# A convolution and attention kernel: the branches' sum gets its own tile, and two readers of GpSimd's results move back in the queue

## The chip, the cores and the metric

The kernel runs on one core of a Trainium2 chip. The metric is the device time of one execution in microseconds (us), the median of several. A core has five engines that matter here, each with a queue of its own that it works off in order: PE (TensorE, matrix products), DVE (VectorE), ACT (ScalarE), POOL (GpSimd) and SP (SyncE, which here only issues DMAs). An instruction whose inputs or whose buffer are not ready waits, and everything behind it on its engine waits with it.

## The reference

The input x is (8, 256, 64, 64) in f32. Two layers follow one another, each on a group-normalised x and with a residual sum. Layer 0 makes 3x3 weights for every point out of 1x1 convolutions and sums nine shifted value maps with them. Layer 1 adds two things: a 7x7 local attention, and a dynamic convolution, nine branches of two depthwise 3x3 convolutions, weighted by a softmax over the branches:

```python
wts = jnp.einsum('oc,bchw->bohw', Wfc, x).reshape(b, C, kc2, h, w)
wts = jax.nn.softmax(wts, axis=2)
...
hid = jax.nn.relu(_dwconv(xr, w1))
oc = _dwconv(hid, w2).reshape(b, kc2, C, h, w)
out_conv = jnp.sum(oc * wts.transpose(0, 2, 1, 3, 4), axis=1)
return rate1 * out_att + rate2 * out_conv
```

The nine branches of the reference are equal before they are weighted, since xr is x broadcast to nine copies. The kernel computes the depthwise result oc once for each channel. It computes eight exponentials of differences to the ninth branch's logits, with S their sum, and multiplies oc by (S + 1) / (S + 1), which in this case is 1 up to rounding. The change leaves all of this arithmetic as it is.

## The kernel before, in words

An image has eight bands of eight rows (512 points); a band has its 256 channels in two halves (ct = 0, 1) of 128 partitions. The main loop goes over the 64 bands g of all images, band by band, and over eight steps s in each band: steps 0 to 3 belong to ct = 0, steps 4 to 7 to ct = 1. A step of layer 1 treats two 8x8 tiles of queries for its half: scores (L699, on PE), masked maxima (L708, DVE), exponentials (L716, ACT), the reciprocal of their sums (L723, DVE), probabilities (L725, ACT), transposes (L731, PE, and L733, ACT), weighted values (L743, PE), and their addition to the output tile xr (L753, DVE). The scores and the weighted values of a step lie in one PSUM tile with the tag "sco", which has one buffer: the next step's scores need L753 to be done.

The same step computes two of the eight branches' logits (L821, PE) and exponentials (L826, ACT) into the two planes of an "ex" tile, tag "ex" with three buffers. POOL sums these tiles over the four steps of a half (L1017, after the second, third and fourth step). DVE works off the depthwise taps of the same half (L778, L804), eight per convolution.

At the end of a half, ACT copies the depthwise result from PSUM to a tile "oc" (L814), and dynamic_sum finishes the half: POOL adds the two planes (L832), DVE adds 1 and caps (L839), takes the reciprocal in two parts (L840, L844), POOL weighs (L849 to L851: sum by reciprocal, oc by that, added to xr), and after the second half SP stores xr.

While layer 1 works on band g, layer 0 prepares the bands g + 10 to g + 12: small_maps and value_maps (PE, and ACT in step 0 and 1), hidden maps, and tap_weights, whose nine products per band are made by DVE (L451) and summed by POOL (L461), two buffers of the tag "prod". The last product's sum is added to the band of x (L464), and "take" measures its statistics (L491, DVE, two bn_stats) and stores it as x1. The first layer's bands run out ten bands before the end.

The order of all queues is written out by hand. A step has six places. Code that stands in the step itself is issued at its place, and `after(n, f)` issues f n places later, ahead of what the step issues there, and in the order in which such calls were made:

```python
def after(n, f):
    later.append((place[0] + n, f))
```

Places are only an order in the queues; nothing waits for a place. In a band of 48 places, counted from step 0: ex tiles are added at places 14, 20 and 26 for the first half and at 38, 44 and 50 for the second (50 is place 2 of the next band). L832 stands at 26 and 50, behind the ex add there. The quotient (L839, L840) stands five places on, at 31 and 55 (step 5 and step 1, place 1 of the step: ahead of two taps and of L723), the second reciprocal (L844) at 34 and 58, the weighing at 36 and 60, the store at 66. The products 0 to 8 stand at 12, 13, 18, 24, 25, 28, 36, 37 and 42, each followed at once by POOL's add (product 0 has none). The copy of old keys (L628, POOL) stands at 14 and 38, the position sums (L616, POOL) at 32; in the bands next to an image's border these come one step earlier. The statistics of take stand seven places after product 8, at 49, which is place 1 of step 0 of the next band.

Of the kernel before, what the change touches and what calls it, by code (L numbers as in the profile page):

```python
# [10 lines left out]
F32 = mybir.dt.float32  # L11
# [7 lines left out]
P = 128  # L19
# [5 lines left out]
BAND = R * W  # L25
# [61 lines left out]
def conv_layers_kernel(ctx: ExitStack, tc: tile.TileContext, ins: dict, out: bass.AP):  # L87
    nc = tc.nc
# [93 lines left out]
    w1 = ctx.enter_context(tc.tile_pool(name="l1", bufs=2))  # L182
# [32 lines left out]
    def after(n, f):  # L215
        later.append((place[0] + n, f))
# [148 lines left out]
    def pieces(v, q):  # L365

        return v.rearrange("(g s) n -> g s n", s=SHARE)[:, :, q * PIECE : (q + 1) * PIECE]
# [61 lines left out]
    def tap_weights(b, i, u, alone, at):  # L429


        im = images[b]
        pw = ps.tile([P, TG, SR * HP], F32, tag="gen", name=f"pw_{b}_{i}_{u}", bufs=5)
        for j in range(TG):
            nc.tensor.matmul(  # L435
                pw[:, j], c2[:, TG * u + j], h2n[i % 2].rearrange("p r c -> p (r c)"), start=True, stop=True
            )

        def product(j):
            k = TG * u + j  # L440
            if alone and j == TG - 1:
                prod = w1.tile([P, NCT, RP, W], F32, tag="yp", name=f"prod_{b}_{i}_{k}", bufs=3)
                prod = prod.rearrange("p t r c -> p (t r c)")[:, : SHARE * SR * HP]
                prod = prod.rearrange("p (s n) -> p s n", s=SHARE)
            else:
                prod = w0.tile(
                    [P, SHARE, SR * HP], F32, tag="prod" if k else "sum", name=f"prod_{b}_{i}_{k}",
                    bufs=2 if k else 1,
                )
            at = k // 3 * HP + k % 3  # L450
            nc.vector.scalar_tensor_tensor(  # L451
                prod[:, :, :RUN], pw[:, j, :RUN].unsqueeze(1).to_broadcast([P, SHARE, RUN]),
                par[:, PCB2 + k : PCB2 + k + 1],
                im.x3q[i].rearrange("p s r c -> p s (r c)")[:, :, at : at + RUN], ALU.add, ALU.mult,
            )
            if k == 0:
                im.sum = prod
            elif alone and j == TG - 1:
                after(5, lambda: gather(prod))
            else:  # L460
                nc.gpsimd.tensor_add(im.sum[:, :, :RUN], im.sum[:, :, :RUN], prod[:, :, :RUN])  # L461
            if k == KK - 2 + (not alone):
                x = im.xg[i]
                nc.gpsimd.tensor_add(x, x, rows(im.sum))  # L464
                if alone:
                    after(8, combine)
                after(20 if alone else 7, take)

        def rows(v):
            return v.rearrange("p s (r c) -> p s r c", c=HP)[..., :W]  # L470

        def gather(prod):
            if u == 0:
                im.part = score_tile(f"sum_{b}_{i}").rearrange("p t (s r c) -> p t s r c", r=SR, c=W)
            for t in range(2):
                nc.tensor.matmul(
                    im.part[:, t], ident, rows(prod)[:, t * SHARE // 2 : (t + 1) * SHARE // 2],
                    start=(u == 0), stop=(u == KK // TG - 1),
                )

        def combine():
            x = im.xg[i].rearrange("p s r c -> p (s r c)")
            nc.vector.tensor_add(x, im.part.rearrange("p t s r c -> p (t s r c)"), x)

        def take():
            x = im.xg[i]
            if i == 0:
                im.st1 = stat.tile([P, 2 * NB, 6], F32, tag="st1", name=f"st1_{b}")
            for t in range(2):
                v = x[:, t * SHARE // 2 : (t + 1) * SHARE // 2].rearrange("p s r c -> p (s r c)")  # L490
                nc.vector.bn_stats(im.st1[:, 2 * i + t, :], v)  # L491
            t = im.x1[i] = dram.tile([C, BAND], F32, tag="x1", name=f"x1_{b}_{i}")
            for q in range(NQR):
                v = x[q * REL : (q + 1) * REL].rearrange("p s r c -> p s (r c)")
                nc.sync.dma_start(out=pieces(t, q), in_=v)

        for j, n in enumerate(at):
            after(n, lambda j=j: product(j))
# [186 lines left out]
    def score_tile(nm):  # L685

        return ps.tile([P, 2, 512], F32, tag="sco", name=f"sco_{nm}")
# [25 lines left out]
    def exponentials(nm, prob, nmax):  # L713
        tot = w1.tile([P, 2], F32, tag="tot", name=f"tot_{nm}", bufs=4)
        for h in range(2):
            nc.scalar.activation(  # L716
                prob[:, h, :NKEY], prob[:, h, :NKEY], AF.Exp, bias=nmax[:, h : h + 1], scale=-1.0,
                accum_out=tot[:, h : h + 1],
            )
        return tot  # L720
# [89 lines left out]

    def depthwise_end(b, i, ct, acc):

        oc = w1.tile([P, BAND], F32, tag="oc", name=f"oc_{b}_{i}_{ct}")
        nc.scalar.activation(oc, acc.rearrange("p r c -> p (r c)"), AF.Copy, scale=rate2)  # L814
        return oc

# [10 lines left out]

    def dynamic_sum(b, i, ct, ex, oc):

        tot = ex[:, 1]  # L830
        xr = images[b].xr[i]
        nc.gpsimd.tensor_add(tot, tot, ex[:, 0])  # L832
        rec = w1.tile([P, BAND], F32, tag="rec", name=f"rec_{b}_{i}_{ct}", bufs=1)
        n = BAND // 2

        def quotient():


            nc.vector.tensor_scalar(tot, tot, 1.0, 1.0e37, ALU.add, ALU.min)  # L839
            nc.vector.reciprocal(rec[:, :n], tot[:, :n])  # L840
            after(3, second)

        def second():
            nc.vector.reciprocal(rec[:, n:], tot[:, n:])  # L844
            after(2, weigh)

        def weigh():

            nc.gpsimd.tensor_mul(tot, tot, rec)  # L849
            nc.gpsimd.tensor_mul(oc, oc, tot)  # L850
            nc.gpsimd.tensor_add(xr[:, ct], xr[:, ct], oc)  # L851
            if ct == NCT - 1:
                after(6, store)

        def store():
            nc.sync.dma_start(
                out=out[b].rearrange("(t p) n -> p t n", p=P)[:, :, i * BAND : (i + 1) * BAND], in_=xr
            )

        after(5, quotient)  # L860


    def beside(g, s):
# [93 lines left out]
    with tc.manual_schedule():  # L957
# [20 lines left out]
        for g in range(-AHEAD, B * NB):  # L978
            b, i = divmod(g, NB)
            for s in range(STEPS):  # L980
                ct, m = divmod(s, NT // 2)
                mid, end = beside(g, s)
                steer(g, s)
                if g >= 0:
# [4 lines left out]
                    tot = exponentials(nm, prob, nmax)  # L989
                advance()  # L990
                if g >= 0:
                    ex, exb = w1.tile([P, 2, BAND], F32, tag="ex", name=f"ex_{nm}", bufs=3), ex if m else None
# [21 lines left out]
                if g >= 0:  # L1014
                    branch_weights(b, i, ct, m, 1, ex)
                    if exb is not None:
                        after(4, lambda ex=ex, exb=exb: nc.gpsimd.tensor_add(ex, ex, exb))  # L1017
                    if m == 1:
                        conv[1]()
                        conv = depthwise_middle(b, i, ct)  # L1020
                    if m == NT // 2 - 1:
                        oc = depthwise_end(b, i, ct, conv[1])
                        after(4, lambda a=(b, i, ct, ex, oc): dynamic_sum(*a))
# [93 lines left out]
```

## Time and profile before

The median of three runs is 4419.8 us (4418.06 to 4427.21). The profiled execution has a span of 4415.5 us at a granted TensorE clock of 0.989.

| engine | busy | share of the span |
|---|---|---|
| PE, matmuls | 4191.5 us | 95% |
| PE, weight loads | 2116.2 us | 48% |
| DVE | 3586.4 us | 81% |
| ACT | 3041.2 us | 69% |
| POOL | 3005.2 us | 68% |

The DMA engines are busy for about a third of the time, and the data comes from HBM at 82 GB/s over the span. Layer 1 begins about 300 us into the span. Between 330 and 3330 us PE is busy for about 974 of every 1000 us; from 3860 us on, where layer 0's products have run out, for 536 of 540 us, and POOL falls from 72% to 48% of the time.

| group | engine | count | mean of one |
|---|---|---|---|
| L461 product into the sum, 128x1040 | POOL | 485 | 2412 ns |
| L1017 ex tiles, 128x1024 | POOL | 384 | 2361 ns |
| L832, L849, L850, L851, 128x512 | POOL | 128 each | 1269 to 1276 ns |
| L839 sum plus one, capped, 128x512 | DVE | 128 | 1123 ns (median 423, longest 3076) |
| L840, L844 reciprocals, 128x256 | DVE | 128 each | 1753, 1746 ns |
| L491 statistics, 128x512 | DVE | 128 | 684 ns |
| L451 product, 128x1040 | DVE | 576 | 1280 ns |

How to read this: a group's mean counts only the time in which the instruction ran, not the time for which it waited. What an engine waited for stands in the list of waits and, in the timeline, in brackets behind an instruction: the idle time of the engine just before it and the instruction that ended it. Bands are nearly equal in length: 64.9 us for bands 1, 2, 4 and 5 of an image, 72.0 for band 0, 67.6 for band 3 (where the next image's weights of layer 0 are scaled), 62.9 and 63.4 for bands 6 and 7, by the starts of the first score matmuls.

### The profile page before, as it was taken

The page shows a single profiled execution, that of the slowest core. Times are in us where ns is not written, and L with a number is a line of the kernel's source. Part 1 is how long each engine was busy: PE and PEld are TensorE (multiplying, and loading weights), DVE is VectorE, ACT ScalarE, POOL GpSimd, SP SyncE. Part 2 cuts the span into 40 slices and gives each one's busy share as a digit, 9 for nine tenths or more (in the row PEclk, how much of TensorE's full clock was granted, in tenths as well). Part 3 has the DMA queues.
Part 4 walks back from the last instruction along what each step waited for, and adds up shares of the span by engine and source line. Part 5 has one row for each costly group of instructions (what it writes and reads, how often), then busy time and mean ns, then how long its engine had stood idle before and what let it go on. Part 6 is the DMA issues. An engine that isn't in the chain of part 4 may idle for free.

```text
span 4415.5 us, 72043 instructions
## 1 busy us (share of the span) xinstructions
PE 4191.5 (95%) x25004; PEld 2116.2 (48%) x25004; DVE 3586.4 (81%) x7244; ACT 3041.2 (69%) x7598; POOL 3005.2 (68%) x1778
## 2 busy tenths in 40 slices
PE   5679999999999999999999999999999999999998
PEld 2334445544454444544445444554445444454444
DVE  5658888888888888888888888888888888877777
ACT  2246777776677776777777676776777776677776
POOL 3657767677777677767777776767777777844444
PEclk9889999999999999999999999999999999999999
DMA  6662423423332332333332342342332332211100
GB/s 190 155 155 69 104 69 78 109 80 76 101 88 70 101 90 69 98 95 77 88 91 77 88 104 63 82 110 69 84 92 60 80 95 56 55 43 34 37 29 20
DMA packets 381259, 367.90 MB, mean 83 GB/s; under 512 B 55392, under 2 KB 282720, under 8 KB 380640
## 3 DMA queue, kind: packets, MB, share of 16 engines
q1 hardware_dynamic: 377568, 358.68, 31.6%
q8 instruction: 198, 3.24, 0.3%
q10 hardware_dynamic: 3328, 4.62, 0.3%
q14 instruction: 165, 1.35, 0.1%
HBM read 261.48 MB, written 101.71 MB: 82 GB/s over the span
## 4 chain that ended last, share of the span: by engine, by line
PE 60%; DVE 18%; POOL 11%; issue 4%; ACT 1%; DMA 1%; SPq 0%; POOLq 0%; DVEq 0%; ACTq 0%
PE pf L821 27%; POOL prod L461 6%; PE sco L743 5%; PE pk L653 4%; PE p L357 4%; DVE prod L451 4%; PE ptp L731 4%; PE sco L699 4%; PE pq L632 3%; POOL ex L1017 3%; DVE acc L778 3%; PE pvt L602 3%; DVE ex L839 2%; DVE acc L804 2%; PE p L325 2%
## 5 line engine op out<-in xcount | busy, mean ns | idle before, releaser
L821 PE MATMUL pf<-yp,c_wfc 128*128 128x512 f32 x4096 | 1988.2, 608 | 1.4
L461 POOL TENSOR_TENSOR prod<-prod,prod 128x1040 f32<-128x1040 f32 x485 | 1170.1, 2412 | 238.7 <-DVE prod L451 212.1
L826 ACT ACTIVATE ex<-pf 128x512 f32<-128x512 f32 x1024 | 606.7, 592 | 545.5 <-PE pf L821 309.2
L1017 POOL TENSOR_TENSOR ex<-ex,ex 128x1024 f32<-128x1024 f32 x384 | 906.7, 2361 | 75.7 <-ACT ex L826 71.0
L821 PEld LDWEIGHTS pf<-yp,c_wfc 128*128 128x128 f32 x4096 | 698.5, 190 | 534.9 <-issue 490.8
L778 DVE SCALAR_TENSOR_TENSOR acc<-yp,c_chan,acc 128x504 f32<-128x504 f32 (+3 forms) x1104 | 765.0, 693 | 55.3 <-ACT acc L769 35.0
L451 DVE SCALAR_TENSOR_TENSOR prod<-pw,c_par,x3q 128x1040 f32<-128x1040 f32 x576 | 733.8, 1280 | 71.2 <-PE pw L435 29.2
L849 POOL TENSOR_TENSOR ex<-ex,rec 128x512 f32<-128x512 f32 x128 | 163.4, 1276 | 902.7 <-DVE rec L844 845.2
L804 DVE SCALAR_TENSOR_TENSOR acc<-hid,c_chan,acc 128x504 f32<-128x504 f32 (+3 forms) x1024 | 757.8, 740 | 18.6 <-ACT acc L798 0.6
L725 ACT ACTIVATE prob<-prob,tot 128x196 f32<-128x196 f32 x1024 | 411.8, 451 | 400.6 <-DVE tot L723 400.6
L716 ACT ACTIVATE prob<-prob,nmax 128x196 f32<-128x196 f32 x1024 | 462.0, 455 | 96.8 <-DVE nmax L708 96.3
L743 PEld LDWEIGHTS sco<-pt,vt 112*64 112x64 f32 x8176 | 282.0, 137 | 368.0 <-issue 126.7
L753 DVE SCALAR_TENSOR_TENSOR xr<-sco,bv,xr 128x128 f32<-128x128 f32 x511 | 174.5, 341 | 309.2 <-PE sco L743 309.0
L708 DVE CUSTOM_DVE_ANT_0 prob<-sco,c_mask 128x196 f32<-128x196 f32 x1024 | 324.3, 354 | 77.8 <-PE sco L699 76.9
L743 PE MATMUL sco<-pt,vt 112*64 112x64 f32 x8176 | 350.9, 228 | 35.0 <-DVE nmax L708 32.7
L699 PE MATMUL sco<-kb,qb 64*64 64x196 f32 x4096 | 295.1, 357 | 51.3 <-DVE xr L753 51.0
L731 PE MATMUL ptp<-ident,prob 128*112 128x128 f32 x2044 | 332.3, 285 | 0.0
L733 ACT COPY pt<-ptp 112x512 f32<-112x512 f32 x511 | 295.6, 579 | 30.1 <-PE ptp L731 29.9
L731 PEld LDWEIGHTS ptp<-ident,prob 128*112 128x112 f32 x2044 | 206.7, 133 | 152.3 <-issue 82.8
L558 PE MATMUL pv<-yp,c_wv 128*128 128x512 f32 (+2 forms) x576 | 251.7, 562 | 0.0
L653 PE MATMUL pk<-yp,c_wk 128*128 128x512 f32 (+2 forms) x576 | 245.0, 553 | 0.0
L357 PE MATMUL p<-xc,w3s 128*128 128x512 f32 x512 | 244.9, 602 | 0.0
(134 smaller groups left out, 5527.6 us busy)
## 6 DMA issues: line engine op xcount, KB each, us to landing
x<-x3n SPq DMA_DIRECT2D x128, 264.0 KB, 2.1
x3q<-x SPq DMA_DIRECT2D x128, 264.0 KB, 6.9
xc<-in_x SPq DMA_DIRECT2D x64, 512.0 KB, 5.3
xg<-in_x SPq DMA_DIRECT2D x256, 128.0 KB, 5.1
x<-xg SPq DMA_DIRECT2D x256, 128.0 KB, 2.4
yp<-x SPq DMA_DIRECT2D x128, 256.0 KB, 3.2
xr<-x SPq DMA_DIRECT2D x64, 512.0 KB, 5.7
out_x<-xr SPq DMA_DIRECT2D x64, 512.0 KB, 3.1
```

Source lines behind the costliest of these rows:

```text
L451: nc.vector.scalar_tensor_tensor(prod[:, :, :RUN], pw[:, j, :RUN].unsqueeze(1).to_broadcast([P, SHARE, RUN]), par[:, PCB2 + k : PCB2 + k + 1],
L461: nc.gpsimd.tensor_add(im.sum[:, :, :RUN], im.sum[:, :, :RUN], prod[:, :, :RUN])
L653: nc.tensor.matmul(pk[:, :n], wk[:, kt, ct * P : (ct + 1) * P], im.yp[i][:, kt, a : a + n], start=(kt == 0), stop=(kt == NCT - 1),)
L699: nc.tensor.matmul(sco[half[t], h, :NKEY], qb[half[h], 2 * m + t].rearrange("p r c -> p (r c)"), kb[half[h], :, c0 : c0 + KW], start=True, ...
L716: nc.scalar.activation(prob[:, h, :NKEY], prob[:, h, :NKEY], AF.Exp, bias=nmax[:, h : h + 1], scale=-1.0, accum_out=tot[:, h : h + 1],)
L731: nc.tensor.transpose(ptp[:, h, ch], prob[:, h, ch * CHUNK : (ch + 1) * CHUNK], ident)
L743: nc.tensor.matmul(po[half[h], :, t * TQ : (t + 1) * TQ], im.vt[i + ch, m][:n, t, (2 * ct + h) * HD : (2 * ct + h + 1) * HD], pt[:n, h, ch ...
L778: nc.vector.scalar_tensor_tensor(o, yp[:, ct, ra + dr : rb + dr, ca + dc : cb + dc], chan[:, ct, CW1 + k : CW1 + k + 1], o, ALU.mult, ALU.add,
L804: nc.vector.scalar_tensor_tensor(o, hid[:, ra + dr : rb + dr, ca + dc : cb + dc], chan[:, ct, CW2 + k : CW2 + k + 1], o, ALU.mult, ALU.add,)
L821: nc.tensor.matmul(pf, wfc[:, kt, 2 * m + j, ct * P : (ct + 1) * P], images[b].yp[i][:, kt, PAD : PAD + R], start=(kt == 0), stop=(kt == N ...
L826: nc.scalar.activation(ex[:, j].rearrange("p (r c) -> p r c", r=R), pf, AF.Exp)
L1017: after(4, lambda ex=ex, exb=exb: nc.gpsimd.tensor_add(ex, ex, exb))
```

## The change

The sum of the two planes goes into a tile of its own, "sumex", with one buffer, instead of the second plane of the ex tile. So the ex tile is no longer held until the weighing. To pay for the new tile, "oc" has one buffer instead of two. The quotient is issued seven places after L832 instead of five, and the second reciprocal, the weighing and the store, which are counted from it, two places later as well. In the main part of the program the statistics of x1 are issued eleven places after the last product instead of seven. The aim is that DVE finds the results of POOL ready when it comes to them and does not stand at the head of its queue waiting.

In places: the quotient comes to 33 and 57 (place 3 of steps 5 and 1: behind two taps and L723, ahead of L753), the second reciprocal to 36 and 60 (ahead of products 6 and 0, which were the next DVE work behind it already), the weighing to 38 and 62 (behind the adds of products 6 and 7 and the ex add at 38, and behind the add of product 1 and the ex add at 14), the store to 68, the statistics to 53 (place 5 of step 0).

```diff
@@ tap_weights, product
-                after(20 if alone else 7, take)
+                after(20 if alone else 11, take)
@@ depthwise_end
-        oc = w1.tile([P, BAND], F32, tag="oc", name=f"oc_{b}_{i}_{ct}")
+        oc = w1.tile([P, BAND], F32, tag="oc", name=f"oc_{b}_{i}_{ct}", bufs=1)
@@ dynamic_sum
-        tot = ex[:, 1]
+        tot = w1.tile([P, BAND], F32, tag="sumex", name=f"sumex_{b}_{i}_{ct}", bufs=1)
         xr = images[b].xr[i]
-        nc.gpsimd.tensor_add(tot, tot, ex[:, 0])
+        nc.gpsimd.tensor_add(tot, ex[:, 1], ex[:, 0])
@@ dynamic_sum, end
-        after(5, quotient)
+        after(7, quotient)
```

## The prediction

> **What bounds the kernel now.** I read the page first (who is busy), then the list of waits, then the timeline of one band, queue by queue.
>
> ```profile
> PE 4191.5 (95%) x25004; PEld 2116.2 (48%) x25004; DVE 3586.4 (81%) x7244; ACT 3041.2 (69%) x7598; POOL 3005.2 (68%) x1778
> ```
>
> PE is the bound by busy time; what can still be won is its holes. The list of waits ("engine line <- what ended the wait: us in total, times, longest") names those that the change touches:
>
> ```profile
> POOL ex L849 <- DVE rec L844: 845.2, 115, 15.6
> ...
> ACT ex L826 <- POOL ex L1017: 202.6, 102, 2.3
> ...
> DVE st L491 <- POOL xg L464: 123.6, 48, 4.1
> ...
> DVE ex L839 <- POOL ex L832: 63.0, 52, 1.7
> ...
> PE sco L699 <- DVE xr L753: 51.0, 43, 1.7
> ...
> ACT ex L826 <- POOL oc L850: 29.8, 60, 1.5
> ```
>
> The edit aims at the third, fourth and sixth. Only the fifth is idle PE time: the score tile has one buffer, so L699 waits until DVE's L753 has read it. Now one ordinary band. POOL from step 1 to step 5:
>
> ```profile
> 2036.72 1.28 POOL L849 TENSOR_TENSOR ex<-ex,rec 128x512 f32<-128x512 f32 x1 [6.97 <-DVE rec L844]
> ...
> 2040.66 2.41 POOL L461 TENSOR_TENSOR prod<-prod,prod 128x1040 f32<-128x1040 f32 x1
> 2043.02 2.38 POOL L1017 TENSOR_TENSOR ex<-ex,ex 128x1024 f32<-128x1024 f32 x1
> ...
> 2052.98 4.88 POOL L461 TENSOR_TENSOR prod<-prod,prod 128x1040 f32<-128x1040 f32 x2 [2.43 <-DVE prod L451]
> 2057.82 2.36 POOL L1017 TENSOR_TENSOR ex<-ex,ex 128x1024 f32<-128x1024 f32 x1
> 2060.26 1.26 POOL L832 TENSOR_TENSOR ex<-ex 128x512 f32<-128x512 f32 x1
> 2061.48 2.40 POOL L461 TENSOR_TENSOR prod<-prod,prod 128x1040 f32<-128x1040 f32 x1
> ```
>
> DVE in step 1, then in step 5, and ACT in step 0:
>
> ```profile
> 2028.70 0.42 DVE L839 TENSOR_SCALAR ex<-ex 128x512 f32<-128x512 f32 x1
> 2029.16 1.75 DVE L840 RECIPROCAL rec<-ex 128x256 f32<-128x256 f32 x1
> ...
> 2032.19 0.16 DVE L723 RECIPROCAL tot<-tot 128x2 f32<-128x2 f32 x1
> 2033.19 0.35 DVE L753 SCALAR_TENSOR_TENSOR xr<-sco,bv,xr 128x128 f32<-128x128 f32 x1 [0.84 <-PE sco L743]
> ...
> 2061.56 2.60 DVE L839 TENSOR_SCALAR ex<-ex 128x512 f32<-128x512 f32 x1 [0.99 <-POOL ex L832]
> ```
> ```profile
> 2024.47 0.60 ACT L826 ACTIVATE ex<-pf 128x512 f32<-128x512 f32 x1 [2.13 <-POOL ex L1017]
> ```
>
> In step 5 the quotient L839 waits 0.99 for L832, then runs 2.60 instead of 0.42, beside the add that POOL began at 2061.48. L753 comes at 2067.29, and PE's L699 has then waited 1.08 (timeline, 2067.68). An ordinary band takes 2061.56 - 1996.65 = 64.91, from one such L839 to the next.
>
> **What the Trainium skill says.** *TensorE: Matmul & The Clock Gate*, on the array's architecture, calls DVE's and ACT's queues strict FIFO. The trace agrees, for POOL too: it sat 6.97 behind L849. *SBUF — State Buffer*, "Who interferes with whom", says that a tensor_scalar in a two-port mode and a GpSimd instruction exclude each other for a whole instruction. The trace agrees: 0.42 alone, 2.60 beside an add of 2.40. *Perfetto Trace Analysis*, "Identifying the Most-Contended Engine", warns that PE's busy share is no distance from its limit; here four 128x512 matmuls take 1.72 from start to start though the page gives 608 ns each. So I count stalls, not busy time.
>
> **The change, part by part.**
>
> *The tile of its own, one oc.* No instruction more or less; L832 writes another address. One 128x512 f32 tile comes and one goes. The buffer of ex is free after L832 and not after L850: that ends 29.8 us of ACT waits, which lie behind PE's matmuls; I count 0. The single oc must be read by L851 before L814 eight places later: by the sums below POOL is about 1 us in time.
>
> *The statistics 7 -> 11.* Two of 0.68 go behind L753 and four or five taps of 0.72, some 4 us, so most of the 123.6 us of DVE waits goes. They lie in step 0, where L723 waits for ACT anyway, and ACT for POOL (2.13). PE has no wait there: 0.
>
> *The quotient 5 -> 7, and behind it second half and weighing.* Places are queue orders, so three orders change.
>
> (1) DVE: quotient (0.46 + 1.67 = 2.13) now stands behind two taps and L723, not ahead of them. In step 5 this is good: 1.43 less between L839 and L753. In step 1 it is bad: L723 can't start before ACT's exponentials, at 2032.19 with or without the quotient ahead of it (ACT's second L716 starts 2031.61, takes 0.45 and 0.19 for the readout). The 2.13 that filled DVE's wait comes behind it.
>
> (2) POOL, step 2: weighing now stands behind the adds of product 1 and of ex. POOL no longer starts at the end of L844 but after DVE's product 0, maxima and product 1: 1.12 + 0.55 + 1.22 = 2.89 later. Behind the waiting add are ex, weighing, kb copy, product 2, ex, and then all that L832 needs; DVE's L839 waits for that.
>
> (3) POOL, step 6: weighing behind products 6, 7 and ex; POOL starts 1.20 later, after product 6. Behind it are the ex adds for whose buffer ACT waits in step 0. The ex add of step 5 comes 3.93 earlier, which ends ACT's wait in step 7; the add that ends the wait in step 0 does not.
>
> These three join up into one ring. Its parts, start to start from the timelines of 1996 to 2067, in the new order:
> - POOL, product 1 to the end of product 5: 2.36 + 2.32 + weighing 3.94 + 0.49 + 2.35 + 2.32 + 4.84 + 2.44 + 1.22 + 2.40 = 24.68
> - DVE, to POOL's product 6: 0.28 until L839 ends, L840 1.70, L753 0.25, taps 1.44, L844 1.67, product 1.20, signal 0.07 = 6.61
> - POOL, product 6 to the ex add of step 6: 4.84 + 2.30 + 3.93 + 0.49 + 2.48 + 2.14 + 2.40 = 18.58
> - ACT, from L826 (2024.47) in queue order to L723 (2032.19): 7.72
> - DVE, L723 to POOL's product 1: 0.08 + 2.13 + 0.27 + 1.43 + 1.67 + 1.12 + 0.55 + 1.22 + 0.07 = 8.54
>
> Sum 66.13. A ring that goes once round per band can't be faster than that: 66.13 - 64.91 = 1.22 more per band. In the old order the same ring has the two POOL parts and ACT unchanged (50.98), 3.6 from L723 over L753, taps and L844 to L849, and 6.93 from product 5 over quotient, taps, L753, taps, L844 to L849: 61.5. That leaves 3.4 of slack, and the trace shows it: POOL idles 2.43 ahead of product 3 and DVE 0.84 ahead of L753, 3.27.
>
> Bands: the ring needs the products and, on ACT, the small maps of the first layer; both run beside images 0 to 5 and beside four bands of image 6.
> - Bands 1, 2, 4, 5 (64.9 each) and 1 to 3 of image 6: 27 x 1.22 = 33.
> - Band 6 (62.9): pe add 0.72 in front of product 5 (2.40 out of the ring), no kb copy in step 6 (0.49): 66.13 - 2.40 + 0.72 - 0.49 = 63.96; 6 x 1.06 = 6.
> - Band 7 (63.4): two kb copies out, pe add 1.30: 64.05; 6 x 0.6 = 4.
> - Band 3 (67.6): bound by the scaling of weights, four tensor_scalars that already wait for POOL's adds (1.09, 2.49, 1.06, 0.34). POOL comes later and they wait for one more add, 0 to 2.4; I take 1.5: 9.
> - Band 0 (72.0): POOL idles 1.95 and 2.98 there, enough for nearly all of the shift; 0 to 1.2, I take 0.5: 7 x 0.5 = 4.
> - The last ten bands have no products: 0.
>
> Together 56: 4420 + 56 = 4475.
>
> **Rivals.** *Faster.* If POOL stays as early as now, L753 comes 1.43 sooner in step 5, more than PE's wait of 1.08: the 51.0 us go, 4420 - 51 = 4369. For it: two of the waits aimed at are as large as meant. Against it: POOL would have to run product 1's add 2.89 before DVE has made it. *Nothing.* If I misjudge the ring by 1.2 of 66, by small pieces of 0.03 over forty instructions or because ACT's freed 2.2 us in step 7 carry over, shift and gain cancel: 4420. *Slower still.* Late ACT also holds PE in steps 1 to 3 (L338 must free a PSUM tile, with 0.76 to spare) and band 3 takes the whole add: 1.6 in each of 54 bands, 4506.
>
> **Numbers.** Ring 0.66, slower still 0.10, nothing 0.06, faster 0.18. The likeliest gives 4475. Low end: 4400, which takes in the case of nothing and a part of the faster one; high end: 4505, the slower still. Faster by over 0.2% 0.18, within 0.06, slower 0.76.
>
> **What would show it.** Ordinary bands of about 66.1; POOL waiting for L451 ahead of product 1's add, and hardly at all ahead of product 3 or L849; DVE idle about 2 us ahead of L723 in step 1; L839 still waiting for L832 in step 5; the wait of L491 gone; PE's waits on L753 as long as now or longer. Wrong if ordinary bands are at 64.9 or below, or if POOL is seen weighing before product 1 is added.

## The result, and the profile after

| | median of 4 runs | lowest to highest |
|---|---|---|
| before | 4419.49 us | 4418.06 to 4427.21 |
| after | 4479.77 us | 4471.14 to 4485.42 |

The ratio is 1.0131, with a 95% interval of 1.0111 to 1.0151: the change makes the kernel slower by about 60 us. Ratios, here and below, are estimated from all executions; the quotient of the medians can differ from them by about 0.001. The profiled execution after is the shortest of its four (4471.14), so its span is only 54 us longer than that of before.

The page of the kernel after, part 1 (busy time of each engine) and part 4 (shares of the chain of work that ended last):

```profile
PE 4217.9 (94%) x25004; PEld 2114.0 (47%) x25004; DVE 3606.9 (81%) x7244; ACT 3057.3 (68%) x7598; POOL 3003.5 (67%) x1778
...
PE 31%; POOL 23%; DVE 22%; issue 9%; ACT 9%; DMA 1%; SPq 0%; POOLq 0%; DVEq 0%; ACTq 0%
```

Of the kernel before, part 4, and from its list of waits the entry for POOL's adds of products:

```profile
PE 60%; DVE 18%; POOL 11%; issue 4%; ACT 1%; DMA 1%; SPq 0%; POOLq 0%; DVEq 0%; ACTq 0%
```
```profile
POOL prod L461 <- DVE prod L451: 212.1, 87, 6.3
```

Part 1 says almost nothing: every engine has as many instructions as before, and its busy time is within 0.7% of that of before. Part 4 says where the time went. Before, the chain ran through PE for 60% of the span, and through DVE, POOL and ACT for 30%. Now it runs through PE for 31%, and through POOL, DVE and ACT for 54%. The chain has left the engine that was the bound.

The list of waits of the kernel after (engine, line, what ended the wait: us in total, times, longest):

```profile
POOL prod L461 <- DVE prod L451: 967.4, 139, 13.0
...
ACT ex L826 <- POOL ex L1017: 169.7, 85, 3.7
...
DVE sumex L839 <- POOL sumex L832: 48.5, 37, 2.5
PE sco L699 <- DVE xr L753: 45.7, 52, 2.6
```

The waits that the change aims at are down: L491's is 1.4 us in all (123.6 before), L850 ends no wait of ACT any more (29.8 before), L839's went from 63.0 to 48.5. What took their place stands at the top: POOL waits 967.4 us for DVE's products, 212.1 before. It used to spend most of that time in front of the weighing L849 (845.2 before, 3.9 now). POOL is idle little longer than before (1466 us against 1410); but it now idles in front of another instruction, and what is queued behind that one is not the same.

One ordinary band on POOL, from the add of product 1 in step 2 to the same add one band later:

```profile
2002.38 2.40 POOL L461 TENSOR_TENSOR prod<-prod,prod 128x1040 f32<-128x1040 f32 x1 [10.95 <-DVE prod L451]
2004.74 2.36 POOL L1017 TENSOR_TENSOR ex<-ex,ex 128x1024 f32<-128x1024 f32 x1
2007.06 1.27 POOL L849 TENSOR_TENSOR sumex<-sumex,rec 128x512 f32<-128x512 f32 x1
...
2023.43 1.27 POOL L832 TENSOR_TENSOR sumex<-ex 128x512 f32<-128x512 f32 x1
2024.66 2.39 POOL L461 TENSOR_TENSOR prod<-prod,prod 128x1040 f32<-128x1040 f32 x1
...
2033.65 4.90 POOL L461 TENSOR_TENSOR prod<-prod,prod 128x1040 f32<-128x1040 f32 x2 [5.42 <-DVE prod L451]
...
2049.86 4.79 POOL L1017 TENSOR_TENSOR ex<-ex,ex 128x1024 f32<-128x1024 f32 x2
...
2068.45 2.40 POOL L461 TENSOR_TENSOR prod<-prod,prod 128x1040 f32<-128x1040 f32 x1 [10.96 <-DVE prod L451]
```

2068.45 - 2002.38 = 66.07 us: one turn. POOL stands still 10.95 us ahead of product 1. For the last 3.0 of them the weighing, which lies behind it, is ready, since L844 ends at 1999.41. Once POOL has begun it has no idle time up to the end of product 5 at 2027.05. On DVE ahead of this product 1, then in step 5 and in step 1 of the next band:

```profile
1997.66 1.75 DVE L844 RECIPROCAL rec<-sumex 128x256 f32<-128x256 f32 x1
...
2024.73 2.60 DVE L839 TENSOR_SCALAR sumex<-sumex 128x512 f32<-128x512 f32 x1 [1.25 <-POOL sumex L832]
...
2059.93 0.17 DVE L723 RECIPROCAL tot<-tot 128x2 f32<-128x2 f32 x1 [2.65 <-ACT prob L716]
2060.01 0.41 DVE L839 TENSOR_SCALAR sumex<-sumex 128x512 f32<-128x512 f32 x1
2060.45 1.75 DVE L840 RECIPROCAL rec<-sumex 128x256 f32<-128x256 f32 x1
```

In step 1 DVE idles 2.65 for ACT, and the quotient (2.11 up to L753), which used to fill that time, comes after it. In step 5 the quotient is two places later and still waits for L832, because POOL has come later too. And L839 still takes 2.60: POOL had begun product 5's add at 2024.66, 0.07 ahead of it. The section "Who interferes with whom" of *SBUF — State Buffer* in the Trainium skill says of a DVE instruction in a two-port mode and a GpSimd instruction that the one which issues first keeps the other out for its whole length; here L839 ends 0.28 after that add. On ACT, in step 0:

```profile
2052.25 0.60 ACT L826 ACTIVATE ex<-pf 128x512 f32<-128x512 f32 x1 [3.28 <-POOL ex L1017]
```

This wait was 2.13; it is longer by 1.15, with the ex add behind the weighing. With that the ring is closed in the trace, and each of its parts can be measured in one and the same band, end to end: POOL from product 1 to the end of product 5, 24.67; DVE to product 6, 6.60; POOL to the end of the ex add of step 6 (2052.22), 18.57; ACT to L723, 7.71; DVE to product 1, 8.52. The sum is 66.07.

What PE loses in this band stands in its timeline:

```profile
2029.35 0.58 PE L699 MATMUL sco<-kb,qb 64*64 64x196 f32 x8 [1.33 <-DVE xr L753]
...
2045.33 0.57 PE L699 MATMUL sco<-kb,qb 64*64 64x196 f32 x8 [0.40 <-POOL kb L628]
```

The first wait is that of the score tile; the second, for POOL's copy of old keys, wasn't in the prediction.

Typical lengths of the bands of one image, by the starts of the first score matmuls:

| band | 0 | 1, 2 | 3 | 4 | 5 | 6 | 7 | image |
|---|---|---|---|---|---|---|---|---|
| before | 71.97 | 64.91 | 67.6 | 64.91 | 65.1 | 62.9 | 63.43 | 526 |
| after | 71.08 | 66.06 | 70.35 | 64.55 | 66.55 | 66.16 | 64.99 | 535.8 |

Six images at +10 us are the 60 us; the seventh, with products beside half of its bands, adds 3. In the two profiled executions themselves these six are 50 longer together, not 60, since in that of before the very first band (76.47) and band 3 of two images (72.29 and 68.96) were longer than usual. The last image, which has no products, is as long as before: 60.82 for its first band and 54.7 for each of the five that follow, in both kernels.

### The profile page after: what moved, and what is told of

Read it like the earlier page. It is cut to its first block, busy times and chain, and to the rows that moved or that the text cites. A ratio compares the mean times of both kernels' runs of the same rounds, so it can differ in the third digit from the quotient of the medians.

```text
span 4469.4 us, 72008 instructions
## 1 busy us (share of the span) xinstructions
PE 4217.9 (94%) x25004; PEld 2114.0 (47%) x25004; DVE 3606.9 (81%) x7244; ACT 3057.3 (68%) x7598; POOL 3003.5 (67%) x1778
## 4 chain that ended last, share of the span: by engine, by line
PE 31%; POOL 23%; DVE 22%; issue 9%; ACT 9%; DMA 1%; SPq 0%; POOLq 0%; DVEq 0%; ACTq 0%
PE pf L821 14%; POOL prod L461 10%; POOL ex L1017 6%; DVE prod L451 6%; PE pk L653 3%; DVE sumex L839 3%; PE sco L743 3%; DVE acc L804 3%; PE ptp L731 2%; POOL xg L464 2%; DVE acc L778 2%; DVE rec L840 2%; PE sco L699 2%; PE pq L632 2%; DVE prob L708 1%
## 5 line engine op out<-in xcount | busy, mean ns | idle before, releaser
L461 POOL TENSOR_TENSOR prod<-prod,prod 128x1040 f32<-128x1040 f32 x485 | 1168.6, 2409 | 1002.1 <-DVE prod L451 967.4
L778 DVE SCALAR_TENSOR_TENSOR acc<-yp,c_chan,acc 128x504 f32<-128x504 f32 (+3 forms) x1104 | 775.9, 703 | 88.9 <-ACT acc L769 68.6
L743 PE MATMUL sco<-pt,vt 112*64 112x64 f32 x8176 | 352.2, 228 | 45.7 <-DVE nmax L708 43.3
L753 DVE SCALAR_TENSOR_TENSOR xr<-sco,bv,xr 128x128 f32<-128x128 f32 x511 | 166.1, 325 | 270.8 <-PE sco L743 270.1
L699 PE MATMUL sco<-kb,qb 64*64 64x196 f32 x4096 | 294.4, 357 | 61.6 <-DVE xr L753 45.7
L632 PE MATMUL pq<-yp,c_wq 128*128 128x512 f32 x512 | 242.7, 596 | 2.7 <-ACT x L338 2.7
```

Of the source, the lines that this page charges most:

```text
L699: nc.tensor.matmul(sco[half[t], h, :NKEY], qb[half[h], 2 * m + t].rearrange("p r c -> p (r c)"), kb[half[h], :, c0 : c0 + KW], start=True, ...
L743: nc.tensor.matmul(po[half[h], :, t * TQ : (t + 1) * TQ], im.vt[i + ch, m][:n, t, (2 * ct + h) * HD : (2 * ct + h + 1) * HD], pt[:n, h, ch ...
L778: nc.vector.scalar_tensor_tensor(o, yp[:, ct, ra + dr : rb + dr, ca + dc : cb + dc], chan[:, ct, CW1 + k : CW1 + k + 1], o, ALU.mult, ALU.add,
```

## The experiments

"Theory" is the ring; its main rival to begin with was that the loss comes from the added buffers or the statistics. Every kernel was timed against the kernel before on the same chip; ratios are to that. All but two compute the reference with the same instructions, in another order or with other buffers; the two with a longer copy repeat it and leave nothing out.

### 1. The statistics alone (kernel before plus one edit)

```diff
-                after(20 if alone else 7, take)
+                after(20 if alone else 11, take)
```

> The kernel before with x1's statistics alone moved from 7 to 11 places behind the last product. Ring theory (the loss comes from one closed ring POOL - DVE - ACT that the quotient's new place lengthens): the statistics are no part of the ring and PE has no wait in step 0, so 4420 us, within 5; DVE's waits of L491 for L464 (123.6 us) fall below 20. Rival (DVE standing at the head of its queue costs time wherever it stands): some 0.5 us in each of 54 bands is won, 4393 us or less.

Measured: 4421.24 us against 4420.52; ratio 0.999 (0.9982 to 0.9997). The wait of L491 for L464 is gone from the list, and the time with it is not: 123.6 us of waits on an engine that is not the bound were worth at most 0.2%.

### 2. The tile alone (kernel before plus sumex and the single oc)

```diff
-        tot = ex[:, 1]
+        tot = w1.tile([P, BAND], F32, tag="sumex", ..., bufs=1)
-        nc.gpsimd.tensor_add(tot, tot, ex[:, 0])
+        nc.gpsimd.tensor_add(tot, ex[:, 1], ex[:, 0])
...
-        oc = w1.tile([P, BAND], F32, tag="oc", ...)
+        oc = w1.tile([P, BAND], F32, tag="oc", ..., bufs=1)
```

> The kernel before with the sum in a tile of its own and one oc buffer; quotient and statistics at their old places. Ring theory: no queue's order changes, 4420 us, within 5; ACT's waits for L850 (29.8 us) end without gain. Rival (the single oc buffer or the other buffers hold ACT or POOL up and make the loss): 4440 us or more, with L814 waiting for L851.

Measured: 4420.85 against 4420.52; 0.9997 (0.9988 to 1.0007). ACT no longer waits for L850, L814 doesn't wait for L851, and the time is the same.

### 3. The change without the statistics

```diff
-                after(20 if alone else 11, take)
+                after(20 if alone else 7, take)
```

> The changed kernel with the statistics back at 7 places. Ring theory: the whole loss is here, 4480 us, within 8, ordinary bands of 66.1 us. Rival (the statistics that now stand ahead of step 1's maxima are part of the loss): 4460 us or less.

Measured: 4482.64; 1.0132 (1.0117 to 1.0147). The whole loss is there. With the two runs above, it comes with `after(7, quotient)`. (The quotient at seven places without the tile, and with the weighing behind it, was not run.)

### 4. The change, with the weighing at its old place

The quotient stays at seven; the weighing is issued in the place of L844, which is where it stood before.

```diff
         def second():
             nc.vector.reciprocal(rec[:, n:], tot[:, n:])
-            after(2, weigh)
+            weigh()
```

> The changed kernel with the weighing issued in the place of the second reciprocal instead of two places later, so that POOL again weighs before it adds products 1, 6 and 7; DVE's order stays the changed one. Ring theory: the ring loses 2.89 and 1.20 us, 66.1 becomes 62.1 and no longer binds; what is left is the gain of 1.43 us between L839 and L753 in step 5, which ends PE's waits of 1.1 to 1.7 us there: 4375 us (4360 to 4395), ordinary bands of 63.6 us. Rival (DVE's own order is at fault: the quotient behind L723 makes step 1 late): 4440 us or more.

Measured: 4367.43; 0.9869 (0.9853 to 0.9886), 8 us below what was expected and faster than both kernels. Ordinary bands take 63.43. The list of waits of this kernel:

```profile
POOL sumex L849 <- DVE rec L844: 885.5, 128, 15.6
...
POOL prod L461 <- DVE prod L451: 177.5, 87, 6.2
```

In front of the weighing and the products together POOL waits no less than in the kernel after (1063 us against 971), and most of it in front of the weighing again. So neither the length of POOL's wait nor the quotient's later place costs time by itself. What costs time is which instruction POOL waits in front of.

### 5. POOL's order alone, first attempt

The quotient goes back to five places; the weighing goes to the place that it has in the kernel after.

```diff
-            after(2, weigh)
+            after(4, weigh)
...
-        after(7, quotient)
+        after(5, quotient)
```

> The changed kernel with the quotient back at 5 places (DVE's order as before) and the weighing 4 instead of 2 places behind the second reciprocal, so that only POOL's order is the changed one. Ring theory: the quotient leaves the ring in step 1 (-2.13 us) and two taps and L723 come into it in step 5 (+1.43): 65.4 us for an ordinary band, between before (64.9) and after (66.1); the whole 4440 us (4430 to 4455). Rival (POOL's order alone is the whole loss): 4475 us. Rival (without the quotient's own move POOL's order does nothing): 4420 us.

Measured: 4487.44 against 4418.53; 1.0155 (1.014 to 1.017). That is a miss of 47 us. In the timeline of ACT of this kernel, in step 7:

```profile
2053.63 0.60 ACT L826 ACTIVATE ex<-pf 128x512 f32<-128x512 f32 x1 [3.85 <-POOL ex L1017]
```

The kernel after has no wait for POOL there. The edit hadn't made the order that it was meant to: calls for one place are issued in the order in which they were made, and `after(4, weigh)` was made earlier than the call of the ex add that falls on the same place. So the weighing, 3.9 us, stood ahead of that ex add. It adds a link of its own, and what it shows is mixed with it.

### 6 and 7. The weighing early in one half only

For the second half (ct = 1), which is weighed in step 2 of the next band, behind products 0 and 1; then for the first half (ct = 0), weighed in step 6.

```diff
-            after(2, weigh)
+            if ct == NCT - 1:
+                weigh()
+            else:
+                after(2, weigh)
```
```diff
-            after(2, weigh)
+            if ct == 0:
+                weigh()
+            else:
+                after(2, weigh)
```

> The changed kernel with the weighing issued at once for the second half of the channels only (in step 2, ahead of product 1); in step 6 it stays behind products 6 and 7. Ring theory: the ring loses about 2.8 of 66.1 us, 63.3, just below what PE needs (63.4, seen with the weighing at once in both halves); ordinary bands 63.4 to 63.6, the whole 4375 us (4365 to 4385). Rival (both halves' orders share the loss evenly): about 4420 us.

Measured: 4401.99; 0.9962 (0.9948 to 0.9976), ordinary bands 64.3. The loss is gone and the kernel is faster than before, but by 27 us less than was expected. In the timeline of PE of this kernel, at the start of step 0:

```profile
2014.72 0.57 PE L699 MATMUL sco<-kb,qb 64*64 64x196 f32 x8 [0.38 <-POOL kb L628]
```

The score matmuls wait for POOL's copy of old keys, which is queued behind the late weighing of the first half. The expectation had no such link: with the ring open, the late weighing in step 6 still reaches PE through the copy, 0.4 us in each band. The bands are 0.9 longer than in experiment 4; for the other half of this PE shows no wait, and its cause is not shown.

> The changed kernel with the weighing issued at once for the first half of the channels only (in step 6, ahead of products 6 and 7); in step 2 it stays behind product 1. Ring theory: the ring loses 1.1 of 66.1 us, 65.0 us for an ordinary band, as long as before: 4425 us (4415 to 4440). Rival (one repaired place opens the ring): 4375 us. Rival (shares even): also about 4420 us, but then the run with the other half at once must give the same.

Measured: 4423.26; 1.0008 (1.0 to 1.0017), ordinary bands 65.03 where 65.0 was expected. The ring without the 1.2 us of the weighing in step 6 is as much shorter as the sum says, and is back at the time of the kernel before. That the two times agree is chance, since single bands differ (band 0 takes 70.5 here and 71.97 before). The halves do not share the loss evenly: against experiment 4, the late weighing of the second half alone costs 56 us here, and that of the first half alone cost 35 us in experiment 6.

### 8. Two edits only

The kernel before, with the quotient two places later and the weighing where it was; no tile, two oc, statistics at seven.

```diff
-            after(2, weigh)
+            weigh()
...
-        after(5, quotient)
+        after(7, quotient)
```

> The kernel before with two edits only: the quotient at 7 places and the weighing issued at once with the second reciprocal; no tile of its own, two oc buffers, statistics at 7. Ring theory: the tile takes no part, POOL frees the ex buffer by L850 in the same order as before, ACT's small waits for L850 stay and cost PE nothing: 4367 us, within 8. Rival (the tile is what lets the later quotient pay): 4390 us or more.

Measured: 4365.79; 0.9879 (0.9865 to 0.9894). The interval overlaps that of experiment 4, so the tile and the statistics are not needed for the gain. PE's waits of L699 for L753, 51.0 us before, are 4.9 here. The timeline of POOL over one band of this kernel:

```profile
1435.25 1.28 POOL L849 TENSOR_TENSOR ex<-ex,rec 128x512 f32<-128x512 f32 x1 [8.06 <-DVE rec L844]
...
1439.19 2.40 POOL L461 TENSOR_TENSOR prod<-prod,prod 128x1040 f32<-128x1040 f32 x1
...
1450.26 4.89 POOL L461 TENSOR_TENSOR prod<-prod,prod 128x1040 f32<-128x1040 f32 x2 [1.18 <-DVE prod L451]
...
1498.54 1.28 POOL L849 TENSOR_TENSOR ex<-ex,rec 128x512 f32<-128x512 f32 x1 [8.06 <-DVE rec L844]
```

The weighing is ahead of product 1, and POOL has slack again, 1.18 ahead of product 3. The busy time by stretches, for this band, and then for the band of the kernel after shown above (length, then busy us and instructions of PE, weight loads, DVE, ACT, POOL, then clock, DMA share and GB/s):

```profile
1435.25:1498.54 63.29, 63.29 (x383) 31.40 (x382) 54.73 (x108) 46.19 (x113) 47.92 (x29) 1.00 0.36 91
```
```profile
2002.38:2068.45 66.07, 63.99 (x383) 31.38 (x382) 55.36 (x108) 46.12 (x113) 47.83 (x29) 1.00 0.35 87
```

The same instructions at the same clock. In the first, PE is never idle; in the second it is idle for 2.08 us. The other 0.70 of the difference of 2.78 is longer busy time.

### 9. POOL's order alone, second attempt

The quotient at five again; the weighing now is called one place later, so that it comes behind the ex add of its place. POOL's order is that of the kernel after.

```diff
-            after(2, weigh)
+            after(1, lambda: after(3, weigh))
...
-        after(7, quotient)
+        after(5, quotient)
```

> The changed kernel with the quotient back at 5 places and POOL's order exactly the changed one (the weighing four places behind the second reciprocal and behind the ex add of that place; in the run with POOL's order only it had stood ahead of that add). Ring theory, corrected by that run: in step 1 DVE now waits for PE's weighted values, which wait for ACT through PSUM (8.28 us from L826 to L753 instead of 7.80), so the ring is 65.43 + 0.5 = 65.9 us and the whole 4465 us (4450 to 4480). Rival (POOL's order costs nothing without the quotient's own move on DVE): 4420 us. Rival (the ex add behind the weighing made that run slow): 4440 us or less.

Measured: 4481.02 against 4418.98; 1.0139 (1.0124 to 1.0154). Ordinary bands take 66.12, 0.2 more than expected, and the time is 1 us above its range. On POOL, ahead of product 1 and of product 6:

```profile
2002.78 2.41 POOL L461 TENSOR_TENSOR prod<-prod,prod 128x1040 f32<-128x1040 f32 x1 [9.46 <-DVE prod L451]
...
2035.60 4.90 POOL L461 TENSOR_TENSOR prod<-prod,prod 128x1040 f32<-128x1040 f32 x2 [6.93 <-DVE prod L451]
```

The quotient's own new place is worth nothing here: against the kernel after, POOL's idle time is 1.51 longer ahead of product 6 (6.93 against 5.42) and 1.49 shorter ahead of product 1 (9.46 against 10.95). The order on POOL alone is the whole loss against the kernel before. It costs more than these 60 us: with the quotient at seven places, experiment 4 is 53 us faster than the kernel before and the kernel after is 112 us slower than experiment 4. The later quotient alone would win these 53 us; the later weighing that comes with it loses twice as much.

### 10 and 11. A longer POOL queue, inside the ring and outside it

The copy of old keys, for one of the two halves, is made three times: in the kernel after, where it lies in the ring, and in the kernel of experiment 8.

```diff
-            nc.gpsimd.tensor_copy(kb[:, : 2 * PAD], im.kb[i - 1, ct][:, R:])
+            for _ in range(1 + 2 * ct):
+                nc.gpsimd.tensor_copy(kb[:, : 2 * PAD], im.kb[i - 1, ct][:, R:])
```

> The changed kernel with POOL's copy of old keys for the second channel half made three times over instead of once (the same copy into the same place): 2 x 0.49 us more of POOL's work per band from image row band 1 on, work that nothing but the queue behind it waits for. Ring theory: it stands inside the ring in bands 1 to 6, so each such band with products takes 0.98 us more: ordinary bands 67.05 us, 39 bands, 4518 us (4508 to 4526). Rival (POOL is busy 67% of the time and its work is hidden; the loss comes from elsewhere): 4480 us, unchanged.

Measured: 4510.29; 1.0209 (1.0192 to 1.0226). Bands 1 and 2 take 67.3 or 67.9; before the extra copies 66.06. The timeline of POOL:

```profile
2027.94 1.73 POOL L629 COPY kb<-kb 128x420 f32<-128x420 f32 x3
2029.63 2.41 POOL L461 TENSOR_TENSOR prod<-prod,prod 128x1040 f32<-128x1040 f32 x1
```

One copy moves the next instruction back by 0.49 (2010.97 to 2011.46 in the kernel after), three by 1.69: 1.20 more, and bands 1 and 2 are longer by 1.2 to 1.8. Not all bands follow: bands 1 to 3 together are 4.0 longer, but bands 4 to 6 only 1.2 together, and bands 7 and 0 are as before. So the whole gains 30 us; 1.2 in each of the 39 bands that the expectation counted would be 47. Why bands 4 to 6 take so little was not tested.

> The same tripled copy in the kernel with the later quotient and the weighing at once (no tile of its own). Ring theory: the ring there is about 62.1 us, with 0.98 more 63.1, still below the 63.4 that PE needs: 4366 us, within 6, as without the copies. Rival (POOL's work costs what it takes wherever it stands): 4405 us.

Measured: 4365.26; 0.988 (0.9866 to 0.9895). The same extra work, in the kernel with the weighing early, costs nothing. This pair is the plainest sign of the ring: the same POOL work costs 30 us of the whole or none, with POOL busy for 68% to 70% of the span in both.

### 12. Band 6: ACT's table loads

Band 6 is 3.2 longer, the largest single error of the sum. In its step 5 the trace of the kernel after shows on ACT:

```profile
2351.47 1.28 ACT L262 ACT_TABLE_LOAD   x1
2352.76 0.20 ACT L262 ACTIVATE sc_b<-sc_b 128x1 f32<-128x1 f32 x1
...
2356.05 1.28 ACT L826 ACT_TABLE_LOAD   x1
```

and on DVE:

```profile
2359.33 0.17 DVE L723 RECIPROCAL tot<-tot 128x2 f32<-128x2 f32 x1 [1.75 <-ACT prob L716]
2359.42 2.60 DVE L839 TENSOR_SCALAR sumex<-sumex 128x512 f32<-128x512 f32 x1
```

The square root for the next image's x1 brings two loads of 1.28 (*ScalarE: Activation LUTs* in the Trainium skill, "What ACT_TABLE_LOAD costs", gives 1283 ns for one). L723 is late by them, and the quotient now stands behind L723. POOL began product 5's add at 2359.34, so L839 runs its 2.60 again. The edit to the kernel after issues the square root five places later, behind the exponentials that this L723 reads:

```diff
         def a4(pg):
             nc.vector.tensor_scalar(sc, pg, GN_EPS, None, ALU.add)
-            after(2, a5)
+            after(7 if name[0] == "b" else 2, a5)
```

> The changed kernel with one more edit: in the norm of x1, the square root of the next image's scale (L262, on ACT) is issued five places later, and all that follows from it in that norm with it. Nothing is left out. In the trace of the changed kernel that square root stands in step 4 of band 6 between ACT's exponentials, and brings two table loads of 1.28 us. ACT's probabilities of step 5 come that much later, L723 waits 1.75 us for them, and the quotient L839, which the change put behind L723, starts at 2359.42, 0.72 after L832 was done at 2358.70, just behind POOL's add of product 5 (2359.34), and takes 2.60 instead of 0.42 to 0.93. With the edit the loads stand behind the exponentials that L723 of step 5 reads. Table-load theory of band 6: L723 comes 2.56 us earlier, ahead of the end of L832; L839 starts at the end of L832, beside the position sums and not beside product 5, and takes under 1 us; four small instructions of that norm (0.5 us together) now stand ahead of L844. From the add of product 1 in band 6 to that in band 7: 66.09 - 0.8 - 1.7 + 0.5 = 64.1 instead of 66.09; six such bands, 11 us less: 4468 (4463 to 4473). Rival, PE theory: band 6 is as long because PE waits for DVE's maxima in steps 6 and 7 (0.99 and 1.10), which the quotient's new place delays whatever ACT does: band 6 stays at 66.1, 4480. Second rival: the table loads are only moved to step 5, hold ACT's exponentials there, and come back in steps 6 and 7: 65.5 to 66, 4477 to 4480.

Measured: 4463.75 against 4424.47; 1.0094 (1.0077 to 1.0111), in the range expected. DVE in step 5 of band 6:

```profile
2357.17 0.93 DVE L839 TENSOR_SCALAR sumex<-sumex 128x512 f32<-128x512 f32 x1 [1.63 <-POOL sumex L832]
```

From product 1 of band 6 to product 1 of band 7 it is now 2399.02 - 2334.81 = 64.21 (66.09 in the kernel after, 64.1 expected). The rival, PE's own waits for maxima, keeps at most the 0.1 that is left. The whole is 16 us shorter than the kernel after; six bands that are 1.88 shorter make 11 of them, and the rest is within the spread of that kernel's four executions (4471 to 4485).

## Why the prediction was right

The forecast was slower, by way of the ring: 4475, measured 4479.77. Step by step:

- **The ring, 66.13.** Measured 66.07 by POOL's product 1, and each of the five parts within 0.02. Right.
- **An ordinary band +1.22.** Measured +1.15 for bands 1 and 2. Right. That the ring is a bound there, not only a sum that fits, is shown by experiments 7, 10 and 11. For bands 4 and 5, where the prediction used the same 1.22, it holds only in the sum (see below).
- **POOL's weighing behind products 1, 6, 7 (parts 2 and 3).** Right: experiments 4, 8 and 9 take this order away or add it alone, and the loss goes and comes with it.
- **The quotient on DVE (part 1), 1.43 good in step 5, 2.13 bad in step 1.** The first measured 1.51, the second 1.49 in the comparison of experiment 9. The second was 0.6 too high: with the quotient gone from behind L723, L753 idles 0.43 before it starts in experiment 9 (none in the kernel after), a wait that the quotient had hidden.
- **Band 6, +1.06.** Wrong in size: +3.2. The step that failed is the sum for this band, which took product 5's 2.40 out of the ring since the position sums stand in front of it. It forgot that L839 now waits for L723, and L723 for two table loads. Experiment 12 gives 64.21 for the ring without them, where the prediction had 63.96.
- **Bands 0, 3, 4, 7.** Forecast +0.5, +1.5, +1.22, +0.6; measured -0.9, +2.75, -0.35, +1.6. Bands 3 and 4 together are +2.4 against 2.7, bands 7 and 0 together +0.7 against 1.1: the sums hold, the split does not. The place of the statistics bears on the split between bands 3 and 4: in experiment 3, which differs from the kernel after in nothing else, they take 68.9 and 66.0 (+1.3 and +1.1), with the same sum. It isn't alone in that, since experiment 12, with the statistics at eleven, has images of both kinds. An image was forecast at +8.5 and is at +10; band 6 alone is 2.1 above its forecast, and the others are 0.6 below theirs together.
- **The tile, the single oc and the statistics at nothing.** Right for the whole (experiments 1, 2 and 3).
- **The signs named.** POOL waits in front of product 1, the wait in step 1 (2.65, about 2 forecast), L839 waiting for L832, L491's wait gone, ACT's wait for POOL in step 7 gone and that of step 0 not: all there. One sign of being wrong was an ordinary band of 64.9 or below; band 4 is at 64.55, but only with band 3 as much longer. PE's waits on L753 "as long or longer" holds only in part: 45.7 against 51.0 in all, with a longest of 2.6 against 1.7. The lost time of PE is spread over more kinds of waits than that.
- **The rival "faster", 4369.** It was tied to one condition, that POOL stays as early as before. Under just that condition (experiment 8) the time is 4365.79, and of the 51.0 us of waits that it counted on, 4.9 are left. Its sum was right, and its condition is what the change doesn't meet.

Three expectations later on failed. In experiment 5 the order that the code makes was not the one meant. In experiment 6 the link from the late weighing over the copy of old keys to PE had been left out, which is half of the miss. In experiment 9 the ring came out 0.2 too short, and the whole 16 us below what was measured. What isn't explained: how the loss divides between bands 7 and 0, what makes it move between 3 and 4, and why bands 4 to 6 hardly follow in experiment 10.

## What to carry to other kernels

When an instruction is moved later, list what moves with it on the other engines, and for each of these what then stands ahead of it in its own queue: here the quotient was moved for DVE's sake, and the weighing, counted from it, fell behind an add that waits 11 us, the last 3 of them with the weighing ready. Then add up the closed ring through the in-order queues, in the order after the change, and compare it with the period of the loop. The busy shares don't show it, since every engine in it has idle time, and the list of waits doesn't either: POOL's waits in front of products and weighing are as long in experiment 4, which is 112 us faster. Here, keeping the consumer at its old place gives 4365.79 us, faster than both kernels, with two edits.

## What the runs showed of the hardware

- Copies of 128x420 on POOL were 0.49 apart from the next instruction when alone and 1.69 for three in a row, 0.60 for each further one.
- The busy time of PE in one band, with the same 383 matmuls recorded at a clock of 1.00, was 63.29 where it never idled and 63.99 where it idled for 2.08. The cause of this was not tested.
